# A four-layer graph network on one Trainium2 core: the third layer's rows of source factors by another queue

## The chip, the cores and the metric

The kernel runs on one core of a Trainium2 chip. The core has TensorE (PE) for matmuls, VectorE (DVE), ScalarE (ACT) and GpSimd (POOL) for elementwise work, and SyncE (SP), which only issues DMAs here. SyncE and GpSimd each hand out their DMAs in the order of their own instruction queue; the transfers themselves run on the core's 16 DMA engines. The metric is the device time of one execution in microseconds, lower being better.

## The reference, cut to what matters

A feature matrix `x` (4096 nodes by 256) goes through four layers over one adjacency matrix `adj` (4096 by 4096, int32), each with a residual sum and a layer norm: a four-head additive attention, a four-head dot-product attention, a single-head additive attention, and a cosine attention. The change concerns the third:

```python
h = x @ W
e_src = h @ a[:D, 0]
e_dst = h @ a[D:, 0]
e = e_src[:, None] + e_dst[None, :]
e = jnp.where(e > 0, e, NEG_SLOPE * e)
att_logits = jnp.where(adj > 0, e, MASK_VAL)
attention = jax.nn.softmax(att_logits, axis=1)
h_prime = attention @ h
return jax.nn.elu(h_prime)
```

Since the slope is under one, `exp` of the leaky sum can be written with factors: apart from a term of the row that the softmax divides out, `exp(leaky(s+d))` is `exp(slope*d) * max(exp(g*s) * exp(g*d), 1)` with `g = 1 - slope`. The kernel keeps `exp(g*s)` in `src`, `exp(g*d)` in `dst`, and multiplies `exp(slope*d)` into the values `V`.

## The kernel before, in words

The nodes are cut into 32 tiles of 128 (`NT`) and 8 blocks of 512 (`NB`, four tiles each). The function `additive_one` is the third layer. It has two kinds of work.

`prepare(b)` makes the operands of block b. `transposed_block` (L118) turns four tiles of `X` on TensorE, with one copy each on VectorE and ScalarE (L119). `additive_values` multiplies them with the weights (L176) and fills `src`, `dst` and `V` (L180 to L183). Then it builds `row`, in which every one of the 128 partitions holds the source factors of all 512 nodes of the block. For block 0 that is done by TensorE: four transposes of a `src` column that is broadcast over 128 columns (L399), in one PSUM bank of the four of pool `gb_ps`, and a copy by ScalarE (L400). For blocks 1 to 7 it goes through DRAM: `src` is stored into a tile `far` in 512 pieces of 4 bytes (L394), then read back and broadcast to all partitions (L395). The read-back needs the store to have landed, so its instruction waits in SyncE's queue.

A unit (b, j) is one block b of 512 source nodes against one tile j of 128 neighbours. `weights` multiplies the block's `row` by `dst` on ScalarE (L409), then applies the adjacency mask on VectorE (L411). The mask comes by SyncE's queue (L407), two units to a tile, in four buffers. `sums` does the four matmuls of the unit (L417), each of which the profile counts as two instructions. Block b's units need row b and no other.

The loop goes over the 256 units with `sums` one unit behind `weights`. During block 0 it calls `prepare(2)` to `prepare(7)`, one in every four units (j = 2, 6, ... 22); blocks 0 and 1 are prepared before the loop. After the third unit comes `tail`, the end of the second layer: two sums on GpSimd (L615), matmuls of them on TensorE (L623 to L637), and the last block's norm. During block 7 the fourth layer's first masks are loaded by GpSimd's queue (L744).

In the first two layers and their parts the order on TensorE is written out by hand. In this layer it is not: a planner orders the instructions of every engine and queue from the program's text and from the times at which it reckons operands to be there. A queue, once ordered, runs strictly in that order.

Of the kernel before, what the change touches and what calls it, by code (L numbers as in the profile page):

```python
# [18 lines left out]
P = 128  # L19
D = 256  # L20
KC = D // P
QB = 4
QW = QB * P
# [5 lines left out]
def kernel(  # L29
# [27 lines left out]
    nc = tc.nc  # L57
# [4 lines left out]
    def pool(stack, name, bufs, **kw):  # L62
        return stack.enter_context(tc.tile_pool(name=name, bufs=bufs, reuse_waits="tile", **kw))
# [48 lines left out]
    def transposed_block(sb, bank, b, copies=(nc.vector.tensor_copy, nc.scalar.copy)):  # L112

        xT = sb.tile([P, KC, QW], FP, name="xT")
        for c in range(KC):
            pt = bank()
            for k in range(QB):
                nc.tensor.transpose(pt[:, k * P:(k + 1) * P], X[:, b * QB + k, c * P:(c + 1) * P], ident)  # L118
            copies[c](xT[:, c, :], pt)  # L119
        return xT  # L120
# [41 lines left out]
    def layernorm_block(b, mv):  # L162
        normalise([X[:, b * QB + k, :D] for k in range(QB)], mv)
# [5 lines left out]
    def additive_values(xT, b, groups, w_sb, V, src, dst, H, slope):  # L169

        g = 1.0 - slope
        heads = "p k (h d) -> p k h d"
        for k, n, pw in groups:
            for c in range(KC):
                for i in range(n):
                    nc.tensor.matmul(pw[:, i, :D + 2 * H], xT[:, c, (k + i) * P:(k + i + 1) * P], w_sb[:, c, :],  # L176
                                     start=(c == 0), stop=(c == KC - 1))
            t = slice(b * QB + k, b * QB + k + n)
            s, d = pw[:, :, D:D + H], pw[:, :, D + H:D + 2 * H]
            nc.scalar.activation(src[:, t, :], s, AF.Exp, scale=g)  # L180
            nc.scalar.activation(dst[:, t, :], d, AF.Exp, scale=g)
            nc.scalar.activation(V[:, t, D:], d, AF.Exp, scale=slope)
            nc.vector.tensor_tensor(V[:, t, :D].rearrange(heads, h=H), pw[:, :, :D].rearrange(heads, h=H),  # L183
                                    V[:, t, D:].unsqueeze(3).to_broadcast([P, n, H, D // H]), OP.mult)

    def add_elu(o, b, k, mv):

        y = X[:, b * QB + k, :D]
        neg = fin1.tile([P, D], FP, name="neg")
        nc.vector.tensor_scalar_min(neg, o, 0.0)  # L190
        nc.scalar.activation(neg, neg, AF.Exp)
        nc.vector.scalar_tensor_tensor(o, neg, -1.0, o, OP.add, OP.max)
        nc.vector.tensor_tensor(y, y, o, OP.add)
        one_row(mv, k, y)
# [169 lines left out]
    def additive_one(w_sb, slope, tail, op, follow):  # L364

        MJ = 2
        mvs, taken = {}, {}
        with ExitStack() as lay:
            keep = pool(lay, "gb_keep", 1)
            V = keep.tile([P, NT, D + 1], FP, name="V")  # L370
            src = keep.tile([P, NT, 1], FP, name="src")
            dst = keep.tile([P, NT, 1], FP, name="dst")
            row = keep.tile([P, N], FP, name="row")
            zp = pool(lay, "gb_z", 3)
            sb = pool(lay, "gb_sb", 2)
            mp = pool(lay, "gb_mask", 4)
            dr = pool(lay, "gb_dram", 2, space=bass.MemoryType.DRAM)

            ps = pool(lay, "gb_ps", 4, space=PSUM)
            pa = pool(lay, "gb_pa", 1, space=PSUM)  # L380
            edges = adjT.rearrange("(t p) i -> p t i", p=P)
            mask, acc, prob = {}, {}, {}

            def bank():
                return ps.tile([P, QW], FP, name="g")

            def prepare(b):
                xT = transposed_block(sb, bank, b)
                groups = [(k, 1, bank().rearrange("p (n f) -> p n f", n=1)) for k in range(QB)]
                additive_values(xT, b, groups, w_sb, V, src, dst, 1, slope)  # L390
                part = row[:, b * QW:(b + 1) * QW]
                if b:
                    far = dr.tile([QB, P], FP, name="far")
                    nc.sync.dma_start(far.rearrange("k p -> p k"), src[:, b * QB:(b + 1) * QB, 0])  # L394
                    nc.sync.dma_start(part, far.rearrange("k p -> (k p)").unsqueeze(0).to_broadcast([P, QW]))  # L395
                    return
                pr = bank()
                for k in range(QB):
                    nc.tensor.transpose(pr[:, k * P:(k + 1) * P], src[:, b * QB + k, :].to_broadcast([P, P]), ident)  # L399
                nc.scalar.copy(part, pr)  # L400

            def weights(b, j):
                cols = slice(b * QW, (b + 1) * QW)
                m = b, j // MJ
                if j % MJ == 0:
                    mask[m] = mp.tile([P, MJ, QW], I32, name="mask")
                    nc.sync.dma_start(mask[m], edges[:, j:j + MJ, cols])  # L407
                e = sb.tile([P, QW], FP, name="e")
                nc.scalar.activation(e, row[:, cols], AF.Relu, bias=-1.0, scale=dst[:, j, :])  # L409
                prob[b, j] = zp.tile([P, QW], FP, name="prob")  # L410
                nc.vector.scalar_tensor_tensor(prob[b, j], e, 1.0, mask[m][:, j % MJ, :], OP.add, OP.mult)  # L411

            def sums(b, j):
                if j == 0:
                    acc[b] = [bank() if b % 2 else pa.tile([P, QW], FP, name=f"acc{k}") for k in range(QB)]
                for k in range(QB):
                    nc.tensor.matmul(acc[b][k][:, :D + 1], prob[b, j][:, k * P:(k + 1) * P], V[:, j, :],  # L417
                                     start=(j == 0), stop=(j == NT - 1))

            def take_all(b):  # L420
                for k in range(QB):
                    rden = fin.tile([P, 1], FP, name="rden1")
                    nc.vector.reciprocal(rden, acc[b][k][:, D:D + 1])
                    taken[b, k] = op.tile([P, D], FP, name="o")
                    nc.vector.tensor_scalar_mul(taken[b, k], acc[b][k][:, :D], rden)

            def outputs(b, k):
                if k == 0:
                    mvs[b] = fin.tile([P, QB, 2], FP, name="mv")
                add_elu(taken[b, k], b, k, mvs[b])  # L430
                if k == QB - 1:
                    layernorm_block(b, mvs[b])

            def even_bank():
                n = next(turn) % QB
                return pa.tile([P, QW], FP, name=f"acc{n}")

            prepare(0)
            prepare(1)
            turn = itertools.count()  # L440
            units = [(b, j) for b in range(NB) for j in range(NT)]
            for i in range(len(units) + 1):
                if i < len(units):
                    b, j = units[i]
                    weights(b, j)
                    if b == 0 and j % QB == 2 and j // QB + 2 < NB:
                        prepare(j // QB + 2)
                if i:
                    b, j = units[i - 1]
                    sums(b, j)  # L450
                    if (b, j) == (0, 2):
                        tail(bank)
                        follow.start()
                    if b and j % 4 == 0 and j // 4 < QB:
                        outputs(b - 1, j // 4)
                    if b == NB - 1 and j in (6, 10, 14):
                        follow.load_mask(0, (j - 6) // 4, prob[b, j][:, :1])

                    if b == NB - 1 and j % 4 == 2 and j // 4 < NB - 2:
                        follow.prepare(even_bank, j // 4)  # L460
                    if j == NT - 1:
                        take_all(b)

        def tail(bank):
            for k in range(QB):
                outputs(NB - 1, k)
        return tail
# [467 lines left out]
```

The softmax here doesn't subtract the row's maximum and nothing guards it: scores larger than these inputs give would overflow.

## Time and profile before

Three runs took 2959.79, 2961.26 and 2964.14 us; the median is 2961.26. The profiled execution took 2961.59 us, with a span of 2959.8 from its first to its last instruction.

| what | where from | value |
|---|---|---|
| TensorE busy, whole span | table of busy time | 2920.2 us (99%) |
| VectorE / ScalarE / GpSimd busy | table of busy time | 66% / 56% / 31% |
| TensorE's share of the chain that ended last | chain | 94% |
| block 0 of the third layer, first L417 to first L417 of block 1 | timeline | 1744.82 to 1847.09 |
| each later block of this layer, from block 2 | chain | 55.51 us |
| stores `far<-src`, SyncE | timeline | 7, from 1745.21 to 1825.44 |
| read-backs `row<-far`, SyncE | timeline | 7, from 1752.64 to 1838.86 |
| GpSimd's last instruction before its next at 2195.15 | timeline | L615, 1745.52 for 2.35 us |

The page gives each group of instructions as line, engine, operation and tiles. The view of waits adds up, for each pair, how long an engine stood idle and what ended it; that of a queue does the same for the instructions that issue DMAs. The chain follows the work that ended last back from the end, at each step to what released it. The view by stretch gives the busy time of every engine between two points, the granted TensorE clock (1.00 is full) and the share of time in which the DMA engines were busy. Matmul ends are modelled, so a busy TensorE is not always one at its peak.

### The profile page before, as it was taken

To read this page: it belongs to the slowest core of one execution; us is meant where nothing else is said; L and a number is where in the kernel's file an instruction comes from. 1 tells how busy PE (TensorE), PEld (TensorE's weight loads), DVE (VectorE), ACT (ScalarE), POOL (GpSimd) and SP (SyncE) were. 2 spreads that over 40 slices of the span, in tenths; PEclk is the share of its full clock that TensorE was granted. 3 is DMA by queue.
4 is the path that set the end of the run, shared out by engine and by line. 5 is a ranking of instruction groups with operands and counts; after the bars stand their busy time and mean duration, and the time that the engine had idled before them with its cause. 6 is when DMAs were issued, how large, how long until landed. Compare 5 with 4: busy or idle time off the path is not lost.

```text
span 2959.8 us, 50964 instructions
## 1 busy us (share of the span) xinstructions
PE 2920.2 (99%) x20587; PEld 1567.0 (53%) x20587; DVE 1940.8 (66%) x2488; ACT 1666.7 (56%) x2605; POOL 920.6 (31%) x635
## 2 busy tenths in 40 slices
PE   9999999999999999999999998999999999999998
PEld 4333333333633333333333366888887777777776
DVE  8899999997467777777877863655655333333333
ACT  7899999996356666666666652444444222222222
POOL 1000100010078888888988840000000000000000
PEclk9999999999999999999999999999999999999999
DMA  7566676764078988888889874555552334443331
GB/s 201 106 134 141 135 143 136 143 123 75 1 161 189 184 180 188 183 183 187 182 183 193 174 159 102 151 153 150 153 139 56 45 57 59 60 60 57 57 57 29
DMA packets 211198, 375.17 MB, mean 127 GB/s; under 512 B 18593, under 2 KB 94353, under 8 KB 210066
## 3 DMA queue, kind: packets, MB, share of 16 engines
q0 software_dynamic: 101632, 176.18, 37.9%
q1 hardware_dynamic: 109056, 195.47, 22.1%
q8 instruction: 161, 2.64, 0.4%
q14 instruction: 75, 0.61, 0.1%
q10 hardware_dynamic: 274, 0.26, 0.0%
HBM read 317.26 MB, written 21.04 MB: 114 GB/s over the span
## 4 chain that ended last, share of the span: by engine, by line
PE 94%; DVE 3%; DMA 2%; ACT 1%; issue 0%; SPq 0%; DVEq 0%; ACTq 0%
PE acc L266 22%; PE acc L806 15%; PE p L581 14%; PE acc L607 14%; PE g L417 7%; PE acc L417 7%; PE p L795 4%; PE g L795 3%; PE g L509 2%; PE g L523 1%; PE g L176 1%; DMA far<-src 1%; PE acc L176 1%; DVE prob L586 1%; PE acc L757 1%; DMA mask<-in_adjT 1%
## 5 line engine op out<-in xcount | busy, mean ns | idle before, releaser
L586 DVE TENSOR_TENSOR prob<-p,mask 128x1024 f32<-128x1024 f32 x512 | 622.4, 1222 | 209.3 <-ACT p L583 206.1
L583 ACT ACTIVATE p<-p,shift 128x1024 f32<-128x1024 f32 x512 | 555.7, 1088 | 338.3 <-PE p L581 337.5
L266 PE MATMUL acc<-prob,V 128*32 128x512 f32 x6144 | 663.8, 592 | 0.0
L593 POOL TENSOR_TENSOR den<-den,prob 128x1024 f32<-128x1024 f32 x248 | 613.7, 2475 | 76.9 <-DVE prob L586 63.7
L255 ACT ACTIVATE prob<-row,dst 128x512 f32<-128x512 f32 x1024 | 635.5, 711 | 0.1
L256 DVE SCALAR_TENSOR_TENSOR prob<-prob,mask 128x2048 f32<-128x2048 f32 x256 | 582.9, 2287 | 25.1 <-ACT prob L255 21.5
L581 PE MATMUL p<-qT,kT 64*64 64x512 f32 x4096 | 531.4, 591 | 6.6 <-DVE prob L586 5.8
L607 PE MATMUL acc<-prob,V 64*64 64x512 f32 x4096 | 530.2, 589 | 3.9 <-DVE kept L612 3.9
L806 PE MATMUL acc<-X,prob 128*128 128x257 f32 x2048 | 485.7, 380 | 0.0
L806 PEld LDWEIGHTS acc<-X,prob 128*128 128x128 f32 x2048 | 388.5, 190 | 162.1 <-issue 114.1
L799 DVE TENSOR_TENSOR prob<-prob,mask 128x512 f32<-128x512 f32 x256 | 176.5, 691 | 420.0 <-ACT prob L798 418.9
L266 PEld LDWEIGHTS acc<-prob,V 128*32 128x32 f32 x6144 | 197.4, 110 | 451.6 <-issue 433.5
L91 POOL COPY tick<-prob 128x1 f32<-128x1 f32 x35 | 41.8, 1193 | 1114.2 <-DVE prob L256 643.8
L409 ACT ACTIVATE e<-row,dst 128x512 f32<-128x512 f32 x256 | 183.6, 721 | 255.1 <-DVE prob L411 227.8
L607 PEld LDWEIGHTS acc<-prob,V 64*64 64x64 f32 x4096 | 155.8, 133 | 289.3 <-issue 278.1
L581 PEld LDWEIGHTS p<-qT,kT 64*64 64x64 f32 x4096 | 153.7, 133 | 288.4 <-issue 260.7
L411 DVE SCALAR_TENSOR_TENSOR prob<-e,mask 128x512 f32<-128x512 f32 x256 | 176.7, 692 | 192.8 <-PE acc L417 82.5
L744 POOL DMA_DIRECT2D mask<-in_adjT x64 | 47.5, 743 | 641.8 <-DVE prob L799 490.8
L417 PE MATMUL g<-V,prob 128*128 128x257 f32 x1024 | 229.0, 382 | 7.9 <-DVE prob L411 7.9
L417 PE MATMUL acc<-V,prob 128*128 128x257 f32 x1024 | 227.3, 382 | 4.9 <-DVE prob L411 4.9
L599 POOL DMA_DIRECT2D den<-prob x240 | 221.3, 922 | 31.0 <-DVE prob L586 25.3
L798 ACT ACTIVATE prob<-p 128x512 f32<-128x512 f32 x144 | 85.7, 596 | 256.8 <-PE p L795 242.9
(149 smaller groups left out, 1956.3 us busy)
## 6 DMA issues: line engine op xcount, KB each, us to landing
mask<-in_adjT SPq DMA_DIRECT2D x256, 512.0 KB
den<-prob POOLq DMA_DIRECT2D x240, 512.0 KB, 5.3
mask<-edges SPq DMA_DIRECT2D x256, 128.0 KB
mask<-in_adjT POOLq DMA_DIRECT2D x64, 512.0 KB, 5.7
edges<-in_adj POOLq DMA_DIRECT2D x32, 512.0 KB, 9.6
den<-prob SPq DMA_DIRECT2D x16, 512.0 KB
row<-far SPq DMA_DIRECT2D x7, 1024.0 KB
X<-in_x SPq DMA_DIRECT2D x7, 512.0 KB
```

The costliest lines, as they stand in the source:

```text
L255: nc.scalar.activation(z[:, h, :], row[b][:, h, :], AF.Relu, bias=-1.0, scale=dst[:, j, h:h + 1])
L256: nc.vector.scalar_tensor_tensor(z, z, 1.0, mask[m][:, j % MJ, :].unsqueeze(1).to_broadcast([P, H, QW]), OP.add, OP.mult)
L266: nc.tensor.matmul(acc[b][h * G:(h + 1) * G, n, :], part, prob[b, j][:, h, :], start=(j == 0), stop=(j == NT - 1))
L417: nc.tensor.matmul(acc[b][k][:, :D + 1], prob[b, j][:, k * P:(k + 1) * P], V[:, j, :], start=(j == 0), stop=(j == NT - 1))
L581: nc.tensor.matmul(p[c * d:(c + 1) * d, r, :], kT[half, c, j * d:(j + 1) * d], qT[half, c, cols], start=True, stop=True)
L583: nc.scalar.activation(p, p, AF.Exp, bias=shift)
L586: nc.vector.tensor_tensor(z, p, mask[m][:, j % MJ, :].unsqueeze(1).to_broadcast([P, KC, QW]), OP.mult)
L593: nc.gpsimd.tensor_tensor(to, to, flat, OP.add)
L599: nc.gpsimd.dma_start(to, flat, accum_op=OP.add)
L607: nc.tensor.matmul(acc[b][r * d:(r + 1) * d, c, :], V[half, j, r * d:(r + 1) * d], prob[b, j][half, r, :], start=(j == 0), stop=(j == NH - 1))
L795: nc.tensor.matmul(p, T[:, 0, j * P:(j + 1) * P], T[:, 1, cols], start=True, stop=True)
L806: nc.tensor.matmul(acc[b][k], prob[b, j][:, k * P:(k + 1) * P], X[:, j, :], start=(j == 0), stop=(j == NT - 1))
```

## The change

The condition under which the row goes through DRAM becomes `b > 1`, so that block 1 falls through to the TensorE way that block 0 takes. For blocks 2 to 7 the store and the read-back are issued on GpSimd's queue. Nothing else differs; the added empty line moves every later line number up by one.

```diff
                 part = row[:, b * QW:(b + 1) * QW]
-                if b:
+                if b > 1:
+
                     far = dr.tile([QB, P], FP, name="far")
-                    nc.sync.dma_start(far.rearrange("k p -> p k"), src[:, b * QB:(b + 1) * QB, 0])
-                    nc.sync.dma_start(part, far.rearrange("k p -> (k p)").unsqueeze(0).to_broadcast([P, QW]))
+                    nc.gpsimd.dma_start(far.rearrange("k p -> p k"), src[:, b * QB:(b + 1) * QB, 0])
+                    nc.gpsimd.dma_start(part, far.rearrange("k p -> (k p)").unsqueeze(0).to_broadcast([P, QW]))
                     return
                 pr = bank()
```

## The prediction

> **What bounds the kernel now.** The page's table of busy time came first, then the chain that ended last in order of time, the queue's own waits, busy time by stretch, and the queue's instructions in order of time. TensorE is called busy for 99% of the span, and the chain is 94% TensorE, so a saving has to come from a place where the chain leaves TensorE. In the third layer it does so at the end of its first block of source nodes (block 0):
>
> ```profile
> 1789.82 6.06 PE acc L417 x28
> 1795.88 14.12 DMA far<-src
> ...
> 1810.93 12.36 DMA mask<-in_adjT
> ...
> 1825.44 13.41 DMA far<-src
> ...
> 1839.29 6.93 DMA mask<-in_adjT
> ...
> 1847.09 57.99 PE g L417 x256
> 1905.08 55.51 PE acc L417 x256
> ```
>
> Columns: start, length, piece, all in microseconds. For 51 us the chain is a ladder of stores into `far` and adjacency loads. The next block then takes 57.99 us where the one after it takes 55.51. Why a `far` store stands before an adjacency load is told by the queue:
>
> ```profile
> SPq L395 <- DMA far<-src: 75.7, 7, 12.3
> ```
>
> (total wait, times, longest.) The instruction that reads `far` back (L395) holds SyncE's queue until the store has landed: seven times, 75.7 us together. What stands behind it, in order:
>
> ```profile
> 1795.88 1.80 SPq L394 DMA_DIRECT2D far<-src  x1
> 1810.02 0.34 SPq L395 DMA_DIRECT2D row<-far  x1
> 1810.45 0.90 SPq L407 DMA_DIRECT2D mask<-in_adjT  x2
> 1811.40 1.04 SPq L394 DMA_DIRECT2D far<-src  x1
> 1824.06 0.34 SPq L395 DMA_DIRECT2D row<-far  x1
> ```
>
> Each round lets two adjacency tiles through, which is four units of work. While a round takes 12 to 14 us that is enough only as long as TensorE also has a `prepare` to do. By stretch (TensorE busy, loads, DVE, ACT, POOL, granted clock, DMA share, GB/s):
>
> ```profile
> 1739.78:1807.20 67.42, 66.28 (x334) 55.80 (x334) 35.90 (x75) 27.51 (x106) 2.35 (x1) 1.00 0.49 100
> 1804.00:1810.00 6.00, 5.10 (x28) 4.20 (x26) 2.52 (x4) 2.00 (x4) 0.00 (x0) 1.00 0.00 0
> 1833.00:1839.00 6.00, 6.00 (x29) 5.08 (x27) 1.11 (x2) 1.75 (x3) 0.00 (x0) 1.00 0.00 0
> 1807.20:1847.09 39.89, 26.20 (x113) 21.27 (x111) 9.61 (x17) 8.46 (x24) 0.00 (x0) 0.89 0.47 107
> 1960.60:2016.11 55.51, 55.51 (x257) 48.58 (x257) 31.36 (x70) 24.67 (x38) 0.00 (x0) 1.00 0.54 152
> ```
>
> Until 1807.20 TensorE is full. After that it is not, and the DMA engines are not the reason: from 1804 to 1810 and from 1833 to 1839 they move nothing at all. The queue is waiting for a receipt. Later blocks draw adjacency tiles faster (152 GB/s) from the same queue without any gap, because no `far` stands in it.
>
> **What the Trainium skill says.** "DMA: Bandwidth & Descriptors", section "Anatomy of one DMA — SWDGE (gpsimd) path", puts most of a small transfer's fixed time, about 2 us, into the write receipt of the target memory, and says that the semaphore wait sits on the issuing sequencer. The trace agrees on the kind and not on the size: a 2 KB `far` takes 7.4 to 14.1 us from issue to the read-back. The same page, "Issuing engines are not separate DMA queues", says that another issuing engine saves only sequencer time. Here exactly that time is short: the waits above are the sequencer's. "SBUF — State Buffer", in its box on DVE blocking DMA, says that writing a GpSimd DMA's descriptors can stand still while VectorE holds the shared port; no row of this third layer shows it, since none of its DMAs is on GpSimd before 2195 us. "TensorE: Matmul & The Clock Gate", Part 1, says that an idle window of about 3.4 us halves the clock until it has been busy for as long. The trace agrees: clock 0.89 after 1807, and block 1, after an idle 7.90 us, is 57.99 - 55.51 = 2.48 us too long.
>
> **The change, part by part.** (1) Removed from SyncE's queue: seven stores and seven read-backs, with the 75.7 us of waits. Adjacency loads then wait for their buffers alone, as they do in later blocks. What TensorE must still do from 1807.20 on: eight transposes 0.87 us, four matmuls 0.87, sixteen of `prepare` 3.66 (the pieces of the round before: 1784.42 to 1789.82), and the other 84 of block 0 at 6.06/28 = 0.2164 us, 18.18. That sums to 23.6 us against the 39.89 it took: 16.3 us of idle and cold time. With block 1's 2.48 the gain is at most 18.8 us. Before 1807.20 at most 67.42 - 66.28 = 1.1 us more lies idle, of which I take nothing: those gaps are waits for VectorE's copies and others.
>
> (2) Added to TensorE: the row of block 1. Its twin in block 0 is four transposes in the chain, 1739.36 for 0.58 us, and they must wait for the last `src` (the row of L399 shows 0.2 us of that). I take 0.6; the bounds are 0.4 and 1.5, the upper one if the extra bank of the four makes the next `prepare` wait for a copy. ScalarE gains one copy, 0.59 us (L400); it is busy 27.51 of 67.42 us in that stretch, so TensorE's work hides it.
>
> (3) Added to GpSimd's queue: six stores and six read-backs. The nearest rows are its adjacency loads (L744, 0.74 us each to issue) and `den` updates (0.92): 12 x 0.8 = 10 us on an engine that is idle from 1747.87 to 2195.15. The six waits for landing now stand there. Behind them on that queue lies nothing of layer three but the cosine adjacency loads at 2196, and ahead of them two sums of `den` (L615). Landing on this queue is not shown for 4-byte pieces: its bulk transfers take 5.3 to 9.6 us, this store from SyncE 7.4 to 14.1; I take 12, with 5 and 24 (one after the other) as bounds. All are far from mattering, since row 2 is first read about 55 us after block 0 ends and each later one another 55 us on. Nothing is charged.
>
> (4) DMA engines: the same bytes, now beside adjacency loads rather than between them: a row is 256 KB, half a tile. At a share of about 0.5 in any stage I charge 0.3 us, bounds 0 and 2.
>
> Sum: 16.3 + 2.5 - 0.6 - 0.3 = 17.9 us off the profiled span of 2959.8, so 2941.9. The three times before have a median of 2961.26; the profiled execution itself stood at 2961.59 by the timer, 1.8 over its span, so I take the gain off the median: 2943.4, rounded to 2943.5.
>
> **Rivals.** *Half the gain.* A second wait stays: TensorE still runs dry once near the end of block 0 because an adjacency tile takes long (the load issued at 1839.29 landed after 6.93 us), or the planner, which orders this layer itself, moves a `prepare`. [...] Against it: four buffers of two units hold 4 x 3.47 = 13.9 us of TensorE's work, and blocks 1 to 7 run so without a gap. One gap of 6.5 us with a cold restart of 2.5 costs 9: 2952.5.
>
> *Slower.* GpSimd's queue takes the place of SyncE's. The second sum of `den` (L615) must precede the matmuls of layer two's end (L623), and TensorE runs in order:
>
> ```profile
> 1745.52 2.35 POOL L615 TENSOR_TENSOR den<-den 128x1024 f32<-128x1024 f32 x1 [7.23 <-DMA den<-prob]
> 1755.61 1.06 PE L623 MATMUL g<-den,ones 64*32 64x512 f32 x8
> ```
>
> In the program's text the store and read-back of block 2 come ahead of that sum. If the planner kept them so, both sums would wait for the landing. That store was issued at 1753.52 in the kernel before, so: 1753.5 + landing + 0.8 of issue + 4.7, against the 1755.6 at which TensorE wants them. With 16 us of landing that is 19.4 us of idle, 2.5 of cold clock, minus the 17.9: 2965.3. It decides from a landing of about 12 us on. Against it: on SyncE the planner put five adjacency loads ahead of block 1's store, which the text has the other way round, so it goes by when operands are ready, and the sum is ready some 8 us before block 2's factors.
>
> *No change.* The adjacency loads, freed, are limited by something that the queue hid: about 2961. Against it: DMA share 0.00 in the waits, and VectorE at 36 of 67 us.
>
> **How the numbers follow.** Two runs of this kernel differ by up to 0.15%, and 0.2% (5.9 us) is about what can be told from no change. The full gain gets 0.80, within 2941 to 2946.5 by the bounds of (2) and (4) and a little from the early gaps. Half the gain, 0.13; no change, 0.03; slower, 0.04. Faster by over 0.2% takes the first two: 0.93. The range runs from 2940.5 up to 2952.5, to the half gain's own figure, which leaves out its upper half and the last two.
>
> **What the profile of the changed kernel would show.** SyncE's queue between 1735 and 1850 holds adjacency loads (and two weight loads) alone, none waiting for `far`; `far<-src` no longer stands in the chain. Block 0's last matmul comes near 1831, block 1 takes 55.5 us with no cold start, and the clock stays at 1.00 between 1807 and 1850. The transposes into `row`'s bank (L399 before, one line further after) count eight. The last two `prepare`s keep their period of 11.5 us. GpSimd waits some 10 us for each `far`, with nobody behind it. Wrong would be: L623 waiting for GpSimd; VectorE's masking (L411, then L412) waiting for `mask` for more than a microsecond or two; or a block after block 0 waiting for its row.

## The result, and the profile after

The changed kernel takes 2944.02 us (median of four runs, 2942.06 to 2944.52) against 2960.88 us of the kernel before on the same chip (2959.79 to 2964.14): a ratio of 0.994, 95% interval 0.9923 to 0.9957. The forecast was 2943.5. The span of the profiled execution went from 2959.8 to 2942.7 us.

The chain that ended last no longer leaves TensorE at the end of block 0 (line numbers from the edit on are one higher than before):

```profile
1801.99 6.07 PE acc L418 x28
1808.06 0.87 PE g L118 x8
1808.93 0.87 PE acc L418 x4
1809.80 3.66 PE g L176 x16
1813.46 18.22 PE acc L418 x84
1831.68 55.51 PE g L418 x256
```

The four lines from 1808.06 to 1831.68 are the four terms of the forecast's 23.6 us, and the block after them takes 55.51 us like all others. By stretch (TensorE busy, loads, DVE, ACT, POOL, clock, DMA share, GB/s):

```profile
1807.90:1831.52 23.62, 23.62 (x114) 20.46 (x113) 10.66 (x20) 9.60 (x24) 1.29 (x2) 1.00 0.78 109
1831.52:1887.03 55.51, 55.51 (x258) 48.58 (x256) 31.37 (x70) 25.60 (x39) 0.54 (x1) 1.00 0.58 173
```

The clock stays at 1.00. The waits between 1735 and 1850, the first two those of SyncE's queue and the third of GpSimd's, show where the landings have gone:

```profile
SPq L408 <- DVE prob L412: 77.2, 16, 7.5
SPq L408 <- DMA mask<-in_adjT: 2.5, 2, 2.1
POOL row L396 <- DMA far<-src: 43.3, 4, 11.7
```

SyncE now waits for VectorE to give a buffer back, which is what a queue of loads that runs ahead should wait for. GpSimd waits up to 13.3 us for a store (the last one, 1817.83 to 1831.91, which the view lists under "issue" and not in this line), where SyncE waited up to 12.3. The order on its queue is the one on which the slower rival turned:

```profile
1746.22 2.35 POOL L616 TENSOR_TENSOR den<-den 128x1024 f32<-128x1024 f32 x1 [8.00 <-DMA den<-prob]
1754.94 0.83 POOL L395 DMA_DIRECT2D far<-src  x1 [6.38 <-ACT V L182]
1765.68 0.56 POOL L396 DMA_DIRECT2D row<-far  x1 [9.90 <-PE acc L418]
```

The second sum of `den` stands ahead of row 2's store, not behind its read-back. (For L396 the view names TensorE as what ended its wait; the read-back uses nothing of TensorE's, so I take this for a store's landing too.)

### The profile page after: what moved, and what is told of

Same layout as the page of the kernel before. It is cut to its first block, busy times and chain, and to the rows that moved or that the text cites. A ratio compares the mean times of both kernels' runs of the same rounds, so it can differ in the third digit from the quotient of the medians.

```text
span 2942.7 us, 50968 instructions
## 1 busy us (share of the span) xinstructions
PE 2915.7 (99%) x20591; PEld 1564.7 (53%) x20591; DVE 1941.6 (66%) x2488; ACT 1668.1 (57%) x2606; POOL 928.5 (32%) x647
## 4 chain that ended last, share of the span: by engine, by line
PE 96%; DVE 3%; ACT 1%; issue 0%; DVEq 0%; ACTq 0%
PE acc L266 23%; PE acc L807 15%; PE p L582 14%; PE acc L608 14%; PE acc L418 8%; PE g L418 7%; PE p L796 4%; PE g L796 3%; PE g L510 2%; PE g L176 1%; PE g L524 1%; PE acc L176 1%; DVE prob L587 1%; PE g L118 1%; PE acc L758 1%; DVE s L138 1%
```

## The experiments

The experiments ran on several chips, and the kernel before took 2956.03 to 2960.43 us beside them, so each is compared with its own. E1 to E8 and E12 have intervals; E9 to E11 are single executions, read by their waits and rates.

**E1, all rows by GpSimd.** In the changed kernel `if b > 1:` becomes `if b:`.

> Rows of all blocks 1 to 7 go through DRAM on GpSimd's queue; block 1's is no longer made by TensorE. Theory (the gain is SyncE's queue freed of the read-backs' waits, the TensorE row only costs 0.6 us): 2943.4 us, 0.6 under the changed kernel. Rival (block 1's row has to come by TensorE, because it is needed first): block 1 begins late, 2950 or more.

Measured: 2943.97 us, ratio 0.9947 (0.9931 to 0.9964). Block 1 begins on time without its row from TensorE. From the end of block 0's row transposes to block 1's first matmul it takes 1831.98 - 1740.47 = 91.51 us, in the changed kernel 1831.68 - 1739.87 = 91.81. TensorE's row for block 1 brings nothing and costs about 0.3 us, too little for the timer.

**E2, only block 1's row by TensorE.** Against the changed kernel, shortened:

```diff
-                    nc.gpsimd.dma_start(far..., src...)
-                    nc.gpsimd.dma_start(part, far...)
+                    nc.sync.dma_start(far..., src...)
+                    nc.sync.dma_start(part, far...)
```

> Only the second part of the change: block 1's row by TensorE, rows 2 to 7 still by SyncE's queue. Theory: the waits of the last three rounds, where TensorE has no prepare to do beside them, stay as they were; 2957 to 2961 us, with the loads of block 0 still late. Rival (the missing first round lets adjacency tiles run ahead for good): 2944 to 2950.

Measured: 2956.73 us, ratio 0.9992 (0.9983 to 1.0): no difference that the timer can tell (the interval reaches 5 us), 0.3 us below what I had expected at least. The waits from 1735 on are still there:

```profile
SPq L396 <- DMA far<-src: 59.2, 6, 12.3
DVE prob L412 <- DMA mask<-in_adjT: 21.3, 4, 6.9
```

Six read-backs hold the queue, and VectorE waits for adjacency tiles. In the profiled execution block 1 begins 1842.62 - 1739.62 = 103.00 us after block 0's row transposes, against 1847.09 - 1739.94 = 107.15 in the kernel before, so up to some 4 us may be this part's own. The rest of the gain belongs to the other part of the change.

**E3, SyncE's queue kept, the read-back moved back in it.** Shortened; each row also has a DRAM tile of its own:

```diff
+                    load = nc.sync.dma_start(mask[m], edges[:, j:j + MJ, cols])
+                    if j == 28 and b + 1 < NB:
+                        with tc.issue_after(load):
+                            nc.sync.dma_start(row[:, (b + 1) * QW:(b + 2) * QW], fars[b + 1]...)
-                    nc.sync.dma_start(part, far...)      # in prepare(b)
```

> All rows 1 to 7 on SyncE's queue as before, but each read-back stands in the queue behind the adjacency load of unit (b-1, 28) instead of right behind its store; seven DRAM tiles instead of two. Theory (the wait at the head of the queue is the whole loss): 2943.5 to 2945 us, no read-back waits for more than 1 us. Rival (stores of 512 pieces of 4 bytes, in flight in the same queue, hold up the landing of adjacency tiles by themselves): half of the loss or more stays, 2951 to 2961.

Measured: 2942.44 us, ratio 0.9945 (0.993 to 0.996). So no second queue is needed. SyncE's queue, in order of time:

```profile
1800.29 0.37 SPq L394 DMA_DIRECT2D far<-src  x1
1803.42 0.37 SPq L406 DMA_DIRECT2D mask<-in_adjT  x1
1803.84 0.97 SPq L409 DMA_DIRECT2D row<-far  x1
1806.96 0.37 SPq L406 DMA_DIRECT2D mask<-in_adjT  x1
```

The read-back at 1803.84 is row 1's, whose store was issued 60 us earlier (1743.91), and holds nobody up. What cost the time was a wait with loads behind it, not the queue's name.

**E7 and E8, where the waits hurt.** Rows 1 to 4 on one queue, rows 5 to 7 on the other; `eng` then issues both DMAs of a row:

```diff
+                    eng = nc.gpsimd if b > 4 else nc.sync     # E7;  E8: if b < 5
```

> Rows 1 to 4 on SyncE's queue as before, rows 5 to 7 on GpSimd's. Theory (a wait costs only where TensorE has less than 12 us of work that needs no new adjacency tile, that is from the store of row 5 on): nearly all of the gain, 2943.4 to 2946 us. Rival (every round takes its share of a deficit that adds up): three of seven, 2952 to 2955.

> The reverse split: rows 1 to 4 on GpSimd's queue, rows 5 to 7 on SyncE's. Theory: adjacency tiles start the last three rounds with their four buffers full, up to two tiles (6.9 us of TensorE's work) better than before, but the three waits stay; 2950 to 2958 us. Rival (a deficit adds up over all rounds): four of seven of the gain, about 2951, with no wait longer than in the kernel before; the two differ in whether rows 5 to 7 alone, moved, give all of it.

Measured: E7 2945.32 us, ratio 0.9954 (0.9939 to 0.9969); E8 2950.49 us, ratio 0.9968 (0.9957 to 0.9979). Moving the last three alone gives nearly everything: 2958.91 - 2945.32 = 13.6 us, where E1 beside it gives 14.9. Moving the first four takes 9.3 us off the 2959.80 beside E8. The two sum to more than all seven give, so each wait does not simply take its own share. E8's time alone could not tell the two theories apart, since both expected about 2951. The early waits cost nothing on the spot, since TensorE has a `prepare` to do in each round, but, as I read it, they use up the head start of the loads: with the head start whole, the last three waits cost less. In E8 VectorE's waits for adjacency tiles in block 0 sum to 9.3 us, in the kernel before to 28.9.

**E4, the rows on ScalarE's queue.** `nc.gpsimd` becomes `nc.scalar` in both lines of the changed kernel.

> As the changed kernel, but stores and read-backs of rows 2 to 7 are issued on ScalarE's queue. Theory (the wait for landing holds up whatever stands behind it, here ScalarE's factor and copy instructions): six waits of 10 us, of which TensorE can cover about 3.5 each with units already made, and cold restarts: 2980 to 2995 us. Rival (only the transfers of adjacency tiles suffer from sharing a queue with the stores): 2944.

Measured: 2990.57 us, ratio 1.0106 (1.0091 to 1.0121). ScalarE's waits from 1738 to 1880:

```profile
ACT e L410 <- DMA far<-src: 50.6, 6, 10.1
```

Six waits again. Here 50.6 us of landing stand in front of the instructions that feed TensorE. From the end of block 0's row transposes to block 1's first matmul it takes 1878.21 - 1740.35 = 137.86 us, 46.05 more than in the changed kernel, so nearly as much comes through. That sum has the slower clock of a restarted TensorE in it (0.992 over the whole run, 0.999 in the changed kernel), which was not taken apart from the waits.

**E5, the slower rival made true.** Layer two's sums of `den` behind row 2's read-back (shortened; `back` holds the read-backs):

```diff
-            join_sums(b, 1, nc.gpsimd)
-            join_sums(b, 2, nc.gpsimd)
+            with tc.issue_after(back[2]):
+                join_sums(b, 1, nc.gpsimd)
+                join_sums(b, 2, nc.gpsimd)
```

> As the changed kernel, but layer two's two sums of den on GpSimd are ordered behind the read-back of row 2, which is the slower rival made true. Read-back issued near 1766, sums done near 1771, TensorE arrives at their matmuls near 1759: 11.5 us idle and a cold restart of 2.5: 2957 to 2959 us. If such a wait were hidden: 2944.

Measured: 2958.25 us, ratio 0.9994 (0.9985 to 1.0002): the whole gain is gone again. TensorE, in order of time:

```profile
1770.13 1.93 PE L625 MATMUL g<-den,ones 64*32 64x512 f32 x8 [11.53 <-POOL den L617]
```

The rival's price was right; with this landing of 10 us (store 1754.13, read-back 1764.73) it would have been no change rather than slower. What decided against it was the planner's order.

**E6, all rows by TensorE.** `if b > 1:` becomes `if b >= NB:`.

> All rows 1 to 7 by TensorE, no far tile and no DMA for rows. Theory: six more sets of four transposes at 0.58 us each on the engine that sets the time, 3.5 us, and up to 0.2 each of waits: 2947 to 2949 us. If the stores on GpSimd still cost the changed kernel something in the adjacency loads: less than that, 2944 or under.

Measured: 2947.67 us, ratio 0.996 (0.9945 to 0.9975). From the end of block 0's row transposes to block 1 it takes 1835.93 - 1740.49 = 95.44 us, 3.63 more than in the changed kernel. Six more sets of transposes at 0.58 are 3.48, so with four buffers the stores cost the changed kernel next to nothing.

**E9 to E11, do the stores hold up the loads themselves?** In E3, E6 and the changed kernel the pool of adjacency tiles gets two buffers instead of four, so that a late tile shows:

```diff
-            mp = pool(lay, "gb_mask", 4)
+            mp = pool(lay, "gb_mask", 2)
```

> The late read-back version (stores on SyncE's queue, no wait for them) with two adjacency buffers instead of four, so that the landing of each tile shows as a wait. Theory A (a store in flight holds back the receipt of adjacency tiles that run beside it): in block 0 single waits of VectorE for a tile reach 8 us or more and the sum of them is at least 15 us above that of the version without stores. Theory B (only the wait of the read-back cost anything): the sum is within 5 us of the version without stores.

> All rows by TensorE, no store at all, with two adjacency buffers instead of four: the yardstick. A tile lands 5 to 7 us after its buffer comes free, against 3.47 us of TensorE's work in the other buffer, so VectorE waits some 2 to 4 us for each tile that has no prepare beside it; by both theories no wait in block 0 over 5 us.

> The changed kernel (stores on GpSimd's queue) with two adjacency buffers instead of four. Theory A, with the hold-up sitting in the DMA engines and not in one queue: waits as with SyncE's stores, at least 15 us over the version without stores in block 0. Theory A, with the hold-up within one queue: as without stores, within 5 us. Theory B: as without stores.

Measured: E9 2961.78 us, E10 2947.07, E11 2960.32. VectorE's waits for tiles from 1736 to 1850, in the order E9, E10, E11:

```profile
DVE prob L414 <- DMA mask<-in_adjT: 23.8, 8, 6.6
DVE prob L412 <- DMA mask<-in_adjT: 1.0, 1, 1.0
DVE prob L412 <- DMA mask<-in_adjT: 27.0, 7, 6.1
```

Without stores two buffers do as well as four (2947.07 against E6's 2947.67); I had expected waits of 2 to 4 us. With stores the sums are 22.8 and 26.0 us higher, on whichever queue the stores are. Single waits reached 6.6 us, not the 8 I had expected. The sums alone leave two other causes open: E10 lacks the read-backs of 256 KB too, and in E9 SyncE's queue also stands still for 31.5 us because the stores wait for ScalarE, with loads behind them. The rates decide. E11 by stretch, in the columns of above, around the store that is issued at 1809.05 and read back at 1821.59:

```profile
1809.00:1812.00 3.00, 3.00 (x15) 2.62 (x15) 1.41 (x3) 0.28 (x1) 0.77 (x1) 1.00 0.93 330
1813.00:1822.00 9.00, 9.00 (x46) 7.63 (x45) 3.67 (x7) 3.16 (x16) 0.41 (x1) 1.00 0.39 34
1823.00:1825.00 2.00, 1.36 (x7) 0.84 (x5) 0.17 (x1) 0.00 (x0) 0.00 (x0) 1.00 0.96 325
```

In the first 3 us after the store's issue the core still moves 330 GB/s. From 1813 to just past the landing it moves 34, although an adjacency load issued at 1812.26 is out, which takes 12.45 us to land. Then it moves 325. Read-backs move in the first and the third stretch alone; without them the loads of the third make 290 GB/s (0.58 MB in 2 us). The next store was issued at 1822.12 and does not show in it yet. E9 has no read-back near its store of 1799.82 (no wait there tells when it landed), and gives the same picture; its next store is issued at 1811.80:

```profile
1804.00:1810.00 6.00, 5.69 (x30) 4.57 (x29) 2.32 (x4) 2.24 (x9) 0.00 (x0) 1.00 0.26 40
1811.00:1813.00 2.00, 2.00 (x11) 1.75 (x10) 1.22 (x3) 0.33 (x4) 0.00 (x0) 1.00 0.99 349
```

So it is the store in flight that slows the loads beside it here. E10, without stores, and below it the changed kernel, with a store out since 1817.83:

```profile
1798.00:1834.00 36.00, 36.00 (x176) 30.67 (x176) 15.03 (x26) 15.05 (x43) 0.00 (x0) 1.00 0.39 113
1823.00:1829.00 6.00, 6.00 (x30) 5.24 (x29) 2.77 (x4) 2.16 (x3) 0.00 (x0) 1.00 0.46 18
```

E10's 113 GB/s is all that block 0 needs, since TensorE is busy throughout. The changed kernel has slow stretches too, 18 GB/s in this one, and TensorE does not feel them: with four buffers it has tiles for 13.9 us of its work in hand and gets over each store. With two it does not.

**E12, the kernel before with a store in four pieces.** Queue, place and wait are as before; `src` is turned first, so that 512 bytes lie together:

```diff
+                    pr = bank()
+                    nc.tensor.transpose(pr[:QB, :P], src[:, b * QB:(b + 1) * QB, 0], ident)
+                    line = sb.tile([QB, P], FP, name="line")
+                    nc.scalar.copy(line, pr[:QB, :P])
-                    nc.sync.dma_start(far.rearrange("k p -> p k"), src[:, b * QB:(b + 1) * QB, 0])
+                    nc.sync.dma_start(far, line)
```

> The kernel before, with SyncE's store and read-back where they were, one behind the other, but the store in 4 pieces of 512 bytes instead of 512 of 4: one transpose by TensorE turns the block's src and ScalarE copies it into a line first, as layer one does it. Theory (the pieces of 4 bytes are what takes long to land and what slows the loads beside them): the read-back waits 1 to 3 us each time instead of up to 12.3, no stall in block 0; seven transposes of one column block at 0.1 to 0.3 us: 2943 to 2946 us. Rival (a small store of this layer lands late whatever its pieces): waits of 7 us and more stay, 2955 to 2961.

Measured: 2942.29 us, ratio 0.9956 (0.9939 to 0.9973). The queue's waits for stores from 1735 to 1850, and a round of it:

```profile
SPq L399 <- DMA far<-line: 4.3, 5, 0.9
```

```profile
1801.22 0.27 SPq L398 DMA_DIRECT2D far<-line  x1
1802.40 0.34 SPq L399 DMA_DIRECT2D row<-far  x1
1803.83 3.92 SPq L411 DMA_DIRECT2D mask<-in_adjT  x2
```

The same 2 KB, on the same queue with the read-back right behind, can be read back 1.2 us after the store's issue instead of 7.4 to 14.1, and the loss is gone without any second queue. The pieces are the root of the wait, and the queue decides only who has to stand it. Their number and their size change together here (512 of 4 bytes, 4 of 512), and were not told apart. The Trainium skill has a place on this: "DMA: Bandwidth & Descriptors", "Rules for kernel authors", says that a non-contiguous last dimension becomes one descriptor per element and is to be rearranged. These runs agree (512 pieces with the strided side, 4 without), and put its price in the third layer at up to 12.3 us of queue per 2 KB.

E1, E3, E12 and the changed kernel cannot be told apart by the timer: their intervals lie over one another.

## Why the prediction was right, and where it was not complete

*The sum.* From the end of block 0's row transposes to block 1 it took 1847.09 - 1739.94 = 107.15 us before and 91.81 after. That is 15.3 us, and block 1 gained 57.99 - 55.51 = 2.48 more: 17.8 against the forecast's 17.9. The spans differ by 17.1, the medians by 16.9; the rest lies elsewhere in the program and within its run to run spread.

*(1) SyncE's queue.* Right: 23.62 us of TensorE's work from the last `prepare` on, against 23.6. E2, E3 and E7 show that the read-backs' waits, with loads queued behind them, were what was taken away.

*(2) The row by TensorE.* 0.58 us in the chain as forecast (0.3 by the difference to E1), and of no use to the time.

*(3) GpSimd.* Twelve issues took 0.76 to 0.83 us for a store and 0.54 to 0.56 for a read-back, 7.9 us together (forecast 10), and up to 13.3 us of waiting each stands where nobody is queued. No later block waited for its row.

*(4) The DMA engines.* The size was right (nothing that shows) and the reasoning was not: the depth of the buffers made it come out so. I charged the new overlap by bytes, but the changed kernel has a DMA share of 0.78 for 109 GB/s, where E10 has 0.39 for 113. And I read the still DMA engines from 1804 to 1810 as a queue that waits, and nothing else. The queue did wait, but an adjacency load was out as well, the second of the pair issued from 1794.93 on, and VectorE got its tile in the midst of that stillness:

```profile
1807.99 1.29 DVE L411 SCALAR_TENSOR_TENSOR prob<-e,mask 128x512 f32<-128x512 f32 x2 [3.37 <-DMA mask<-in_adjT]
```

The tile issued at 1810.93 fared alike: the engines moved 213 GB/s from 1812 to 1818 and 3 from there to 1824, yet it landed at 1823.29. So the ladder in the chain before was two things: loads issued late, behind the read-back, and loads that landed late (12.36 us for this one) beside a store. In these two places the bytes had moved and the landing came late; in E9 and E11 the bytes themselves move slowly. Whether both have one cause was not tried. The changed kernel removes only the loads issued late. The overlap that it adds would have cost the whole gain with two buffers instead of four (E11: 2960.32 us, 2960.43 for the kernel before).

*The rivals.* Half the gain and no change fell with VectorE's waits after, among which no adjacency tile stands between 1735 and 1850. The slower one fell by the planner's order alone; E5 confirms its working.

## What to carry to other kernels

A DMA instruction that waits for another DMA's landing is to be looked at with what is queued behind it: give it a queue on which nothing urgent follows, or issue it later, when its wait is over. Before that, ask why the landing takes long; here 512 pieces of 4 bytes made a 2 KB store into a 7 to 14 us affair, and one small transpose with a copy ended that. A wait costs on the spot only where the engine that sets the time has less work in hand than the wait is long, and what it uses up of that work can be missing at the next one (E7 and E8), so read it at each of its places and not from its sum.

## What the runs showed of the hardware that was not expected

In the stretches read here, a store of 2 KB in pieces of 4 bytes left the loads beside it alone for about 3 us after its issue. Then adjacency loads of 2 KB rows got through at 34 GB/s until it had landed, and at 290 right after (E11); in E9, where its landing does not show, at 40 and then 349. It did so whether it came from SyncE's queue (E9) or GpSimd's (E11). Which part of the way to DRAM is held up was not tried. In pieces of 512 bytes the same store could be read back after 1.2 us (E12).

Two adjacency buffers were enough without such stores (one wait of 1.0 us in block 0, E10), though I had reckoned with a landing of 5 to 7 us for each tile.
